# Mixer attention scores on 64 rows instead of 32, and three shifts in the traced order of a four-layer image kernel

## The chip, the cores and the metric

The kernel runs on one core of one Trainium2 chip. The metric is the device time of one execution in microseconds. TensorE is called PE here, VectorE DVE, ScalarE ACT, GpSimd POOL, and SyncE, which issues the DMAs, SP.

## The reference

Eight images of 256 channels by 32x32 (1024 tokens) go through four layers, each `x = x + layer(group_norm(x))` with 32 groups. Cut to what matters:

```python
# layer 0: attention, 8 heads of 64; q and k have unit length over the tokens
attn = softmax(einsum('bhdi,bhdj->bhij', q, k) * 10.0)
out = einsum('oc,bcxy->boxy', w_out, attn @ v) + b_out
# layers 1 and 2: 3x3 convolutions, 256 -> 256 channels
# layer 3
xn = layernorm(tokens of x)
xm = four branches of 64 channels: mamba(xn) + skip * xn   # a selective scan over the tokens
g  = sigmoid(conv1d(conv1d(xm)));  xg = g * xm
R  = pointwise(depthwise3(xg)) + xg
xm2 = pointwise(depthwise3(concat(x, R))) + x
x_local  = depthwise3(xm2)
x_global = mha(xm2)                                        # 8 heads of 32
t = gelu(layernorm(concat(x_local, x_global) @ fc.T + fc_b))
out = layernorm(depthwise 3x3 of ln_hw(t)) @ proj.T + proj_b
```

## The kernel before, in words

All data are float32, and channels lie on partitions: an image is two tiles of 128 x 1024. A Python program traces all instructions, and a scheduler with priorities then lays them out; each engine runs its own list strictly in that order. An instruction that waits therefore holds everything behind it on its engine.

There are two streams. `scan_layers` is the layer norm and the four scans of image b (64 units; a unit is a `drive` product on POOL, two `decays` on ACT, two `scan` steps on DVE, a `weigh` product on POOL and matmuls `y<-hs,sel` on PE). The other stream, `dense`, does for its neighbours what needs PE: `back_layers` of image b-1 (gate, projections, mixer attention), `front_attention` of image b+1 (layer 0), `back_out` of b-1, then `front_convs` of b+1 (the output projection of layer 0, in `project_both`, and both convolutions) with `back_end` of b-1 among them. `interleave` runs `dense` and sums the costs that it yields; each time the sum passes a multiple of `PACE[b]` (2.95 for most images) it traces one more step of the scans. `held` ties what is traced for the scans to the last dense instruction of the same engine ahead of it. `amid` gives the steps of `back_end` to places in the list of `front_convs`' yields. Those yields are numbered from 0: 0 to 3 are the output projection, 4 the group norm of convolution 1, 5 to 16 its twelve weight loads, 17 the group norm of convolution 2, 18 to 29 its loads.

Image 0's first layers come before the first scan, and the last image's mixer and end come after the last scan. Six stages between have all of the above; the one after them has the scans of the last image and only the mixer and the end of the image before.

An attention is cut in units: `scores` is a pair of heads' matmuls into one PSUM tile `big`, ACT takes `exp` of it into `p`, and two units later `values` multiplies `p` with v into `acc`. There are two `big` tiles and twelve work tiles (pool `tp`) for everything of size 128 x 1026. In layer 0 (`front_attention`) a pair is two heads of 64 rows, so the scores' operands lie on rows 0 to 63 and 64 to 127. In the mixer (`mixer_attention`) a pair is heads i and i+1, with operands of 32 rows:

```python
rows = [slice((j % 4) * 32, (j % 4) * 32 + 32) for j in (i, i + 1)]
...
"q": [qk[t][r, 0:N] for r in rows],
"k": [qk[2 + t][r, 0:N] for r in rows],
```

All four projections q0, k0, q1, k1 (`qk`, four work tiles) are made ahead of the first unit, and the local depthwise convolution (`local`, two work tiles) ahead of the attention. A head's sums and outputs come out of `acc` through `both` and DMAs; the division by the sums is in `invert`.

A group norm takes `channel_stats` on DVE (`st`, `mv`), two small matmuls with `gmat`, a chain of thirteen small DVE operations (`inverse_root`), and two ACT operations that write the padded images `im`. A layer norm over channels takes matmuls with `mean_w`, squares on ACT, the matmuls `acc<-mean_w,ln_sq`, a chain on DVE (`ln_r`) and matmuls with `ident`. In `back_end` the 3x3 depthwise convolution is 16 DVE steps ("taps", `dw<-xo,vec,dw`), followed by a layer norm whose mean is the matmul `big<-dw,mean_w`.

Of the kernel before, what the change touches and what calls it, by code (L numbers as in the profile page):

```python
# [19 lines left out]
P = 128  # L20
# [13 lines left out]
def preact_stack(ctx: ExitStack, tc: tile.TileContext, I, out, cols):  # L34
# [185 lines left out]
    fc_w = wdp.tile([2, P, 4, P], F32, tag="fc_w", name="fc_w")  # L220
    half_d = wp.tile([P, NB], F32, name="half_d")
    vector.tensor_scalar_mul(half_d, vec[:, cols["mD"] : cols["mD"] + NB], 0.5)
    half_qb = wp.tile([P, 2], F32, name="half_qb")
    vector.tensor_scalar_mul(
        half_qb, vec[:, cols["qpwb"] : cols["qpwb"] + 2], 0.5
# [144 lines left out]
    def inner(t):  # L370
        return t[:, 1 : N + 1]
# [683 lines left out]
    def mixer_attention(x2, img, exact=False):  # L1055


        v = vp.tile([P, NKT, 8, 64], F32, tag="v", name="v3")
        vector.memset(v[:, :, :, 32:64], 1.0)
        wv = chunk("ainv", 0)  # L1060
        for kt in range(0, NKT, 4):
            ps = big_tile()
            for i in range(4):
                for c in range(2):
                    tensor.matmul(
                        ps[:, i * C : (i + 1) * C],
                        inner(x2[c])[:, (kt + i) * P : (kt + i + 1) * P],
                        wv[:, c],
                        start=c == 0,
                        stop=c == 1,  # L1070
                    )
            vector.tensor_copy(
                v[:, kt : kt + 4, :, 0:32],
                ps.rearrange("p (k a b) -> p k a b", k=4, b=32),
            )
            yield 3.8

        qk = {}
        for t in (0, 2, 1, 3):
            qk[t] = work("qk3")  # L1080
            w = chunk("ainqk", t)
            ps = big_tile()
            for h in range(2):
                for c in range(2):
                    tensor.matmul(
                        ps[:, HALVES[h]],
                        w[:, c],
                        inner(x2[c])[:, HALVES[h]],
                        start=c == 0,
                        stop=c == 1,  # L1090
                    )
            scale = 32.0**-0.5 if t < 2 else 1.0
            vector.tensor_scalar(
                qk[t][:, 0:N], ps, col("ain_b", t), scale, ALU.add, ALU.mult
            )
            yield 3.4

        o = img["o3"] = [work("o3_0"), work("o3_1")]

        def head(i):  # L1100
            t, rows = i // 4, slice((i % 4) * 32, (i % 4) * 32 + 32)

            def take(half, acc):

                vector.tensor_copy(o[t][rows, half], acc)

            return {
                "q": qk[t][rows, 0:N],
                "k": qk[2 + t][rows, 0:N],
                "v": lambda kt: v[:, kt, i, 0:32],  # L1110
                "rows": rows,
                "take": take,
            }

        if exact:
            attention_exact(head(i) for i in range(8))
            return

        sums = {}

        def pair(i):
            t = i // 4
            rows = [slice((j % 4) * 32, (j % 4) * 32 + 32) for j in (i, i + 1)]

            def v_of(j):
                return lambda kt: v[:, kt, j]

            def take(h, acc, _):
                if t not in sums:
                    sums[t] = dp.tile([4, N], F32, tag="sums4", name="sums")  # L1130
                both = half_work("both")
                scalar.copy(both, acc)
                for e in range(2):
                    j, at = (i + e) % 4, e * 64
                    nc.sync.dma_start(
                        out=o[t][rows[e], HALVES[h]], in_=both[at : at + 32]
                    )
# [4 lines left out]
                if i % 4 == 2 and h == 1:  # L1142
                    ot = o[t][:, 0:N]

                    return invert(
                        sums[t], 4, 32, lambda r: vector.tensor_mul(ot, ot, r)
                    )

            return {
                "q": [qk[t][r, 0:N] for r in rows],  # L1150
                "k": [qk[2 + t][r, 0:N] for r in rows],
                "v": [v_of(i), v_of(i + 1)],
                "take": take,
            }

        yield from attention([lambda i=i: pair(i) for i in range(0, 8, 2)], False)

    def back_layers(img, exact=False, begin=None):

        xm = img.pop("xm")  # L1160

        q4 = work("q4")
        ps = big_tile()
        for h in range(2):
            for j in range(2):
                tensor.matmul(
                    ps[0:96, HALVES[h]],
                    qdw[:, j].rearrange("p k n -> p (k n)"),
                    inner(xm[j])[:, HALVES[h]],
                    start=j == 0,  # L1170
                    stop=j == 1,
                )
# [12 lines left out]
        yield 4  # L1185
        for j in range(2):
            ps = big_tile()
            for h in range(2):
                tensor.matmul(
                    ps[:, HALVES[h]],  # L1190
                    qpr[:, 2 * j : 2 * j + 2].rearrange("q b m -> q (b m)"),
                    q4[0:96, HALVES[h]],
                    start=True,
                    stop=True,
                )

            gate = work("gate")[:, 0:N]
            scalar.activation(
                gate, ps, AF.Tanh, bias=half_qb[:, j : j + 1], scale=0.5
            )  # L1200
            part = inner(xm[j])
            vector.scalar_tensor_tensor(part, gate, 1.0, part, ALU.add, ALU.mult)
        yield 3.4
        xt = load_x(img["xd"])


        rd = [work("rd0"), work("rd1")]
        for t in range(2):
# [12 lines left out]


        xs = [work("xs0"), work("xs1")]
        for t in xs:
            zero_ends(t)
        group_norm(xt, img["stats"], [inner(t) for t in xs])
        fd = []
        for t, src in enumerate(xs + r):
            fd.append(work("fd"))
            depthwise3(fd[t][:, 0:N], src, "fdw_w", "fdw_b", t)  # L1230
        x2 = [work("x20"), work("x21")]
        for t in x2:
            zero_ends(t)

        def evac_x2(m, ps):
            vector.scalar_tensor_tensor(
                inner(x2[m]), ps, col("fpw_b", m), inner(xs[m]), ALU.add, ALU.add
            )

        yield from project("fpw", fd, evac_x2)  # L1240


        local = [work("local0"), work("local1")]
        for t in range(2):
            depthwise3(local[t][:, 0:N], x2[t], "lc_w", "lc_b", t)
        for n, cost in enumerate(mixer_attention(x2, img, exact)):
            yield cost
            if n == 58 and begin is not None:
                next(begin)
        img["mix"] = xt, local  # L1250

    def merge_weights():
# [164 lines left out]
    def amid(stream, other, places):  # L1417
# [6 lines left out]
            yield cost  # L1424
        yield from other

    def slow(stream):

        for cost in stream:
            yield SLOW * cost  # L1430

    SLOW = 0.35
    PACE = [1.8] + [2.95] * (batch - 2) + [1.6]
    imgs = [{} for _ in range(batch)]
    drain(
# [3 lines left out]
    for b in range(batch):  # L1439

        def dense():
# [12 lines left out]
            if front is None:  # L1454
# [147 lines left out]
```

## Time and profile before

| What | Value |
|---|---|
| Time, three runs | 6783.45, 6793.21, 6796.24 us; median 6793.21 |
| Run of the profile | 6773.59 us, span 6771.8 us |
| Granted PE clock over the span | 0.859 |
| POOL products, `drive` and `weigh` | 512 each, 2568 and 2509 ns |
| DVE scan step | 1024, 1207 to 1265 ns |
| ACT `exp` of a unit | 1024, 1020 ns |
| Convolution matmuls | 2304, 1072.6 us busy |

The profile is one execution. Busy times are of an engine; idle time ahead of an instruction is put down to what released it last. The granted clock says what share of the full TensorE clock the chip's throttle let through. One float32 matmul of the source is two instructions in the profile. All instructions on PE, ACT and DVE that go through the kernel's wrapper `Paced` bear its line, L102; they are told apart by the tiles that they write and read.

### The profile page before, as it was taken

Reading aid. Unit: us, or ns where it says so; the run is one execution under the profiler, and the core shown is the slowest. Engines: PE = TensorE matmul, PEld = TensorE weight load, DVE = VectorE, ACT = ScalarE, POOL = GpSimd, SP = SyncE. Lnnn points to the kernel's source line nnn. Section 1 sums busy time; section 2 is a strip of 40 time slices with the busy share of each in tenths; the row PEclk is TensorE's granted clock in tenths of the full one; section 3 lists DMA queues with packets and bytes.
Section 4 is the critical chain, followed back from the end, with each engine's and each line's share of the span. In section 5 each row is a group of like instructions: output and inputs, shape, how many; then the busy total and the mean of one; then the engine's idle time right before and its main releaser. Section 6 shows DMA issues by size and latency. Waiting matters only on the chain.

```text
span 6771.8 us, 52155 instructions
## 1 busy us (share of the span) xinstructions
PE 5753.1 (85%) x17310; PEld 1933.1 (29%) x17310; DVE 3974.1 (59%) x4610; ACT 2690.7 (40%) x3225; POOL 2685.5 (40%) x1297
## 2 busy tenths in 40 slices
PE   8887688987998979998889888898799987978586
PEld 2331133222422234222332223322242223411132
DVE  4257745578545775467744775557854577545532
ACT  3234324543354433544235442454324452334232
POOL 0026652534344352633515334253434534265500
PEclk9987897998988979799888988789888998966697
DMA  1013232322233122221223222232222312223200
GB/s 49 27 59 84 77 83 67 90 57 75 72 89 86 47 76 78 73 80 48 84 66 91 64 62 79 69 87 57 70 77 70 104 39 82 77 69 89 80 19 30
DMA packets 216688, 470.81 MB, mean 70 GB/s; under 512 B 60116, under 2 KB 101716, under 8 KB 214360
## 3 DMA queue, kind: packets, MB, share of 16 engines
q1 hardware_dynamic: 216408, 467.38, 24.4%
q8 instruction: 139, 2.28, 0.1%
q14 instruction: 141, 1.16, 0.1%
HBM read 394.31 MB, written 64.49 MB: 68 GB/s over the span
## 4 chain that ended last, share of the span: by engine, by line
PE 59%; DVE 23%; issue 5%; ACT 5%; DMA 4%; POOL 2%; SPq 1%; DVEq 0%; POOLq 0%; ACTq 0%
PE big L102 37%; PE acc L102 14%; PE da L102 6%; DVE p L102 6%; DVE hs L102 5%; PE y L102 3%; DVE dw L102 2%; DVE t L102 2%; POOL hs L942 1%; DVE u L102 1%; DVE dt L102 1%; POOL hs L974 1%; DMA dt<-dt_m 1%; DVE st L102 1%; ACT p L102 1%
## 5 line engine op out<-in xcount | busy, mean ns | idle before, releaser
L942 POOL TENSOR_TENSOR hs<-du,bc 128x1024 f32<-128x1024 f32 x512 | 1307.7, 2568 | 1632.6 <-DMA dt<-dt_m 1296.5
L974 POOL TENSOR_TENSOR hs<-hs,bc 128x1024 f32<-128x1024 f32 x512 | 1284.3, 2509 | 835.2 <-DVE hs L102 762.5
L102 ACT ACTIVATE p<-big 128x1024 f32<-128x1024 f32 x1024 | 1038.6, 1020 | 1000.8 <-PE big L102 977.4
L102 PE MATMUL acc<-p,v 128*64 128x512 f32 x4096 | 1261.0, 688 | 29.5 <-ACT o L102 27.0
L102 PE MATMUL big<-im,w 128*128 128x512 f32 x2304 | 1072.6, 622 | 54.2 <-ACT im L102 36.7
L102 ACT ACTIVATE da<-dt,a_neg 128x512 f32<-128x512 f32 x1024 | 689.8, 687 | 888.9 <-DVE hs L102 673.0
L102 DVE TENSOR_TENSOR p<-p 128x1024 f32<-128x1024 f32 x448 | 793.0, 1770 | 296.9 <-ACT p L102 169.7
L102 DVE TENSOR_TENSOR_SCAN hs<-da,carry,hs 128x512 f32<-128x512 f32 x512 | 625.4, 1265 | 332.2 <-POOL hs L942 216.7
L102 DVE TENSOR_TENSOR_SCAN hs<-da,hs 128x512 f32<-128x512 f32 x512 | 598.9, 1207 | 375.9 <-POOL hs L942 221.5
L102 PE MATMUL big<-qk,qk 32*128 32x512 f32 x2048 | 734.6, 769 | 31.5 <-ACT p L102 29.2
L102 PE MATMUL big<-q,k 64*128 64x512 f32 x2048 | 604.6, 661 | 68.5 <-ACT p L102 40.9
L102 PEld LDWEIGHTS big<-im,w 128*128 128x128 f32 x2304 | 448.5, 199 | 696.1 <-issue 615.6
L973 POOL COPY carry<-hs 128x2 f32<-128x2 f32 x256 | 104.7, 409 | 1294.8 <-DVE hs L102 1279.4
L102 PE MATMUL y<-hs,sel 128*32 128x512 f32 x2048 | 409.3, 700 | 204.4 <-POOL hs L974 204.3
L102 PEld LDWEIGHTS acc<-p,v 128*64 128x64 f32 x4096 | 226.6, 146 | 930.0 <-issue 810.1
L102 PEld LDWEIGHTS big<-qk,qk 32*128 32x128 f32 x2048 | 191.2, 216 | 566.6 <-issue 260.6
L102 PE MATMUL big<-xn,w 128*128 128x512 f32 x512 | 255.7, 657 | 60.0 <-DMA w<-in_wqk 29.0
L102 PEld LDWEIGHTS big<-q,k 64*128 64x128 f32 x2048 | 163.1, 191 | 496.2 <-issue 260.2
L102 DVE SCALAR_TENSOR_TENSOR dw<-xo,vec,dw 128x961 f32<-128x961 f32 (+1 forms) x128 | 227.4, 1806 | 29.8 <-ACT dw L102 29.1
L102 PE MATMUL da<-xn,w_minw 64*128 64x512 f32 x256 | 150.7, 705 | 81.5 <-DVE hs L102 80.9
L102 PE MATMUL big<-o,w 128*128 128x512 f32 x384 | 189.6, 646 | 11.4 <-DVE o L102 11.4
L102 DVE SCALAR_TENSOR_TENSOR u<-raw,vec,u 128x1024 f32<-128x1024 f32 x96 | 136.5, 1422 | 106.4 <-ACT u L102 105.2
(205 smaller groups left out, 4975.3 us busy)
## 6 DMA issues: line engine op xcount, KB each, us to landing
bc<-bc SPq DMA_DIRECT2D x1024, 128.0 KB
dt<-dt_m SPq DMA_DIRECT2D x512, 128.0 KB
du<-du_m SPq DMA_DIRECT2D x512, 128.0 KB
w<-in_wc SPq DMA_DIRECT2D x192, 192.0 KB
rs<-inv SPq DMA_DIRECT2D x64, 256.0 KB
dt_m<-dt SPq DMA_DIRECT2D x64, 256.0 KB
du_m<-a SPq DMA_DIRECT2D x64, 256.0 KB
xt<-in_x SPq DMA_DIRECT2D x8, 1024.0 KB
```

The source lines that it names most:

```text
L102: made = issue(*args, **kwargs)
L942: nc.gpsimd.tensor_mul(u["hs"], u["du"], both_groups(u["bc"][:, 0]))
L973: nc.gpsimd.tensor_copy(carry[:, u["q"], g : g + 2], hs[:, :, HALF - 1])
L974: nc.gpsimd.tensor_mul(hs, hs, both_groups(u["bc"][:, 1]))
```

## The change

There are four edits.

- **Masked q, 64 rows.** The mixer makes two copies of q instead of one: `q[0]` holds the even groups of 32 rows and zeros in the odd ones, `q[1]` the reverse (a per-row factor `alt` of the usual scale or zero; DVE writes one copy and ACT the other). A pair is now heads i and i+2, and a score multiplies 64 rows of k, those of two heads, with 64 rows of masked q, of which 32 are zero. The sum is that of one head. The pairs are 0, 1, 4, 5 instead of 0, 2, 4, 6.
- **q and k of the second half later.** `q_and_k(1)` is traced when the attention first asks for pair 4, eight units before it is due, instead of ahead of the attention. The places of `begin` in the list of yields move by the two yields that so go.
- **Local convolution later.** Its two halves are traced at yields 34 and 40 of the mixer.
- **Lull, and a later image end.** `lull` holds back the cost of yields 0 to 3 and 15 to 16 of `front_convs` and passes it on with the next yield, so no scan step is traced there. The steps of `back_end` have new places in the same list.

```diff
-        for t in (0, 2, 1, 3):
-            qk[t] = work("qk3")
...
+        def q_and_k(t):
+            for at in (t, 2 + t):
...
+                if at == t:
+                    q = [work("qk3")[:, 0:N] for _ in range(2)]
+                    vector.tensor_scalar(
+                        q[0], ps, col("ain_b", t), alt[:, 0:1], ALU.add, ALU.mult
+                    )
+                    scalar.activation(
+                        q[1], ps, AF.Identity, bias=alt_b[:, t, 1:2], scale=alt[:, 1:2]
+                    )
+                else:
+                    k = work("qk3")[:, 0:N]
+                    vector.tensor_scalar_add(k, ps, col("ain_b", at))
+                yield 3.4
+            qk[t] = q, k
+        yield from q_and_k(0)
...
+            if t not in qk:
+                drain(q_and_k(t))
+            q, k = qk[t][0][i % 2], qk[t][1]
...
-                "q": [qk[t][r, 0:N] for r in rows],
-                "k": [qk[2 + t][r, 0:N] for r in rows],
-                "v": [v_of(i), v_of(i + 1)],
+                "q": [q[e * 64 : e * 64 + 64] for e in range(2)],
+                "k": [k[e * 64 : e * 64 + 64] for e in range(2)],
+                "v": [v_of(i), v_of(i + 2)],
...
-        yield from attention([lambda i=i: pair(i) for i in range(0, 8, 2)], False)
+        yield from attention([lambda i=i: pair(i) for i in (0, 1, 4, 5)], False)
...
-        local = [work("local0"), work("local1")]
-        for t in range(2):
+        local = []
+        def add_local():
+            t = len(local)
+            local.append(work("local"))
             depthwise3(local[t][:, 0:N], x2[t], "lc_w", "lc_b", t)
         for n, cost in enumerate(mixer_attention(x2, img, exact)):
             yield cost
-            if n == 58 and begin is not None:
+            if n in (34, 40):
+                add_local()
+            if n == 56 and begin is not None:
                 next(begin)
...
+    def lull(stream, spans):
+        owed = 0.0
+        for n, cost in enumerate(stream):
+            if any(a <= n < b for a, b in spans):
+                owed += cost
+                yield 0.0
+            else:
+                yield cost + owed
+                owed = 0.0
...
+    LULLS = (0, 4), (15, 17)
...
             yield from amid(
-                front_convs(imgs[b + 1]),
+                lull(front_convs(imgs[b + 1]), LULLS),
                 back_end(last, out[b - 1]),
-                (0, 4, 6, 7, 8, 9, 10, 11, 12, 13, 14, 16, 17, 20, 22, 25),
+                (5, 6, 8, 9, 10, 11, 12, 13, 14, 15, 16, 18, 20, 22, 24, 26),
             )
```

More of the change, by code (lines that the diff above doesn't have):

```diff
@@ L222, in preact_stack @@
     vector.tensor_scalar_mul(half_d, vec[:, cols["mD"] : cols["mD"] + NB], 0.5)
+    alt = wp.tile([P, 2], F32, name="alt")
+    nc.gpsimd.memset(alt, 0.0)
+    for g in range(4):
+        nc.gpsimd.memset(alt[g * 32 : g * 32 + 32, g % 2 : g % 2 + 1], 32.0**-0.5)
+    alt_b = wp.tile([P, 2, 2], F32, name="alt_b")
+    for t in range(2):
+        vector.tensor_scalar_mul(alt_b[:, t], alt, col("ain_b", t))
     half_qb = wp.tile([P, 2], F32, name="half_qb")
@@ L1078, in mixer_attention @@
         qk = {}
-        for t in (0, 2, 1, 3):
-            qk[t] = work("qk3")
[L1081 to L1090, printed above, removed]
-                    )
[L1092 to L1096, printed above, removed]
+        def q_and_k(t):
+            for at in (t, 2 + t):
+                w = chunk("ainqk", at)
+                ps = big_tile()
+                for h in range(2):
+                    for c in range(2):
+                        tensor.matmul(
+                            ps[:, HALVES[h]],
+                            w[:, c],
+                            inner(x2[c])[:, HALVES[h]],
+                            start=c == 0,
+                            stop=c == 1,
+                        )
[3 more added lines that the diff above has]
+                        q[0], ps, col("ain_b", t), alt[:, 0:1], ALU.add, ALU.mult
+                    )
+                    scalar.activation(
[7 more added lines that the diff above has]
+        yield from q_and_k(0)
         o = img["o3"] = [work("o3_0"), work("o3_1")]
@@ L1105, in take @@
                 vector.tensor_copy(o[t][rows, half], acc)
+            if t not in qk:
+                drain(q_and_k(t))
             return {
-                "q": qk[t][rows, 0:N],
-                "k": qk[2 + t][rows, 0:N],
+                "q": qk[t][0][i % 2][rows],
+                "k": qk[t][1][rows],
                 "v": lambda kt: v[:, kt, i, 0:32],
@@ L1122, in pair @@
             t = i // 4
-            rows = [slice((j % 4) * 32, (j % 4) * 32 + 32) for j in (i, i + 1)]
+            if t not in qk:
+                drain(q_and_k(t))
+            q, k = qk[t][0][i % 2], qk[t][1]
             def v_of(j):
@@ L1133, in take @@
                 for e in range(2):
-                    j, at = (i + e) % 4, e * 64
+                    j, at = i % 4 + 2 * e, e * 64
                     nc.sync.dma_start(
-                        out=o[t][rows[e], HALVES[h]], in_=both[at : at + 32]
+                        out=o[t][j * 32 : j * 32 + 32, HALVES[h]],
+                        in_=both[at : at + 32],
                     )
@@ L1141, in take @@
                     )
-                if i % 4 == 2 and h == 1:
+                if i % 4 == 1 and h == 1:
                     ot = o[t][:, 0:N]
@@ L1247, in back_layers @@
             yield cost
-            if n == 58 and begin is not None:
+            if n in (34, 40):
+                add_local()
+            if n == 56 and begin is not None:
                 next(begin)
+        while len(local) < 2:
+            add_local()
         img["mix"] = xt, local
```

## The prediction

> **What bounds the kernel now.** I read the page first: engines, granted clock, chain.
>
> ```profile
> span 6771.8 us, 52155 instructions
> PE 5753.1 (85%) x17310; PEld 1933.1 (29%) x17310; DVE 3974.1 (59%) x4610; ACT 2690.7 (40%) x3225; POOL 2685.5 (40%) x1297
> PEclk9987897998988979799888988789888998966697
> PE 59%; DVE 23%; issue 5%; ACT 5%; DMA 4%; POOL 2%; SPq 1%; DVEq 0%; POOLq 0%; ACTq 0%
> ```
>
> TensorE (PE) carries the end: 85% busy, 59% of the chain, and not always at full clock (0.859 over the span). DVE is the other 23%. The groups show the two kinds of scores:
>
> ```profile
> L102 PE MATMUL big<-qk,qk 32*128 32x512 f32 x2048 | 734.6, 769 | 31.5 <-ACT p L102 29.2
> L102 PE MATMUL big<-q,k 64*128 64x512 f32 x2048 | 604.6, 661 | 68.5 <-ACT p L102 40.9
> ```
>
> As many matmuls, with as much streamed, cost 130 us more in the mixer (32 rows) than in the image attention (64 rows). By stretch, in this order: a mixer with scans, an image attention, the last mixer with scans, the mixer after the scans, the convolutions. Columns: length, busy time and count of PE, PEld, DVE, ACT, POOL, granted clock, DMA share, GB/s.
>
> ```profile
> 1896.00:2106.00 210.00, 196.22 (x623) 44.23 (x624) 94.04 (x93) 115.19 (x140) 120.78 (x65) 0.80 0.32 88
> 2157.00:2347.00 190.00, 171.41 (x620) 45.38 (x618) 139.54 (x137) 94.71 (x114) 57.48 (x23) 0.97 0.19 53
> 5924.00:6294.00 370.00, 299.68 (x732) 61.03 (x728) 174.33 (x142) 155.10 (x195) 231.11 (x118) 0.66 0.28 76
> 6531.00:6661.00 130.00, 129.68 (x503) 31.42 (x504) 3.00 (x5) 68.04 (x71) 0.00 (x0) 1.00 0.05 12
> 1560.00:1814.00 254.00, 212.52 (x583) 92.97 (x582) 162.37 (x204) 67.52 (x82) 121.30 (x59) 0.86 0.26 79
> ```
>
> The mixer has LESS idle than the attention (13.8 against 18.6 us) and yet a clock of 0.80 against 0.97. With no scans and no idle, 32-row scores keep clock 1.00. So 32 rows are not slow in themselves; they fail to get the clock back once it is lost. One stretch inside the first mixer, then the timeline of each kind at work:
>
> ```profile
> 1906.40:1947.30 40.90, 39.89 (x82) 7.40 (x80) 15.89 (x12) 15.03 (x19) 19.28 (x12) 0.51 0.15 40
> ```
>
> ```profile
> 1909.40 1.98 PE L102 MATMUL acc<-p,v 128*64 128x512 f32 x4
> 1911.30 2.08 PE L102 MATMUL big<-qk,qk 32*128 32x512 f32 x4
> 1913.31 1.98 PE L102 MATMUL acc<-p,v 128*64 128x512 f32 x4
> ```
>
> PE is busy 39.89 of 40.90 us at half clock, a unit (scores and values) taking 3.9 us. The attention at full clock takes 2.07 us a unit (scores 1.06, values 1.01), and mixer units at full clock take the same. The last view is PE in a convolution stage:
>
> ```profile
> 1587.46 0.59 PE L102 MATMUL acc<-mv,gmat 128*128 128x4 f32 x2 [7.92 <-DVE mv L102]
> 1669.77 1.02 PE L102 MATMUL big<-dw,mean_w 128*128 128x512 f32 x2
> 1678.63 3.78 PE L102 MATMUL da<-xn,w_minw 64*128 64x512 f32 x4 [7.84 <-DVE hs L102]
> 1687.69 4.21 PE L102 MATMUL big<-dw,mean_w 128*128 128x512 f32 x6 [5.28 <-DVE dw L102]
> ```
>
> PE waits 7.92 us for the statistics before the first group norm, and 13.1 us in the middle of convolution 1, because the image end's mean matmul stands there before its DVE taps are done.
>
> [...]half-clock spells here last multiples of 3.41 us[...] the spell above lasted 40.96 us, busy throughout.[...] a pair of scores still runs side by side; the trace agrees (four instructions in 1.06 us either way).[...] taps here take 1187 ns at the least and up to 3339.
>
> **The change part by part.** The sum is against the profiled span, 6771.8 us; its run took 6773.6, the three others 6783 to 6796.
>
> 1. *64-row scores.* Removed: nothing on PE, the matmul count stays. Six mixers run beside scans, lasting 210.9, 209.5, 219.5, 219.1, 219.5, 212.8 us between first and last score (mean 215.2). Their full-clock work is (210.0-13.8) x 0.80 = 157 us each. At the attention's clock, a little lower for the scans' waits (0.95), 157/0.95 = 165; plus idle of 22 (now 14 to 17, the attention 18; it grows because POOL, 120 us in 210, has less time): 187. Gain 28 x 6 = 168; bounds 10 and 35 each. The seventh (370.5 us, clock 0.66, 70 idle) is paced by scans: 46 units of scan in it; a stretch of the second mixer did 8 units in 53 us, 6.6 each, so 305 at best, and 325 taken: gain 45, bounds 15 and 65. The last, already at 1.00: nothing.
>    Added: a second masked q copy, on ACT, 2 per image x 8; the nearest PSUM row on ACT (`xo<-big`) is 1.11 us, so 18 us of ACT, which is 40% busy; its reader comes a pair (16 units) later. It holds its PSUM buffer no longer than DVE's 1.28 us copy beside it. Bounds 0 to 1 us each. The setup's five memsets and two small DVE operations lie under the first loads.
> 2. *Second q and k inside the attention.* PE's 7 us are moved, not added; a bubble of about 1 us at the PSUM buffers, as the attention's own waits (16.4 us in 24 on `ACT big`), against 7 us earlier start of exp. The four weight loads stand where they stood on SP. Zero; bounds -1 and +3 per image.
> 3. *Local convolution later.* Four DVE steps of 1.28 and two of 1.24 on ACT leave the start of the mixer, where PE waits 2.76 us for `x`, and go where DVE is under half busy. 2 us x 7 = 14; bounds 0 and 3.
> 4. *Image end later.* The build order shows the mean matmul after convolution 2 has begun, its taps before convolution 1's last statistics. The 13.1 us go. But all 16 taps now lie before those statistics: from the tap start to there DVE has about 29 us of taps (16 x 1.8), 14 of scans, 5 of others, 48, against about 50 of PE work: some of the wait returns at the second group norm, 4 taken. Both `ln_sq` sums leave the group norms' wait, where DVE's chain sat 6.5 us behind them; PE loses that filling (7 us cold), and does it warm elsewhere (32 matmuls took 4.1 us at full clock): +3. On SP the image's load goes five yields later, the stores one; the x buffer they free is wanted one step later than before: bounds 0 to 3.
> 5. *Lull.* Statistics without scans between: the three scan steps (1.2 each) and `dt` ahead of `mv` go: from 8 to about 5 us. Filling for PE is gone, so the two group norms idle 8.5 us each against 16.6 together before: zero. What is held (13.8 and 10.4 of cost, at 2.95 a step 4.7 and 3.5 steps, each with its SP loads, ACT decays, DVE scans, POOL products, PE sums) arrives in a burst: PE sums may wait for POOL: 2 taken, 0 to 20. Parts 4 and 5: 13.1-4+3-2 = 10 us x 6 images = 60; bounds -5 and 20 each.
>
> Sum: 168+45+14+60 = 287, so 6485 by the span; from the median, 6793-287 = 6506. I say 6510.
>
> **Rivals.** *Zeros don't count* (half the masked q is zero[...]): the mixers stay at 0.80, parts 3 to 5 remain: 6793-74 = 6719. For it: the trace has no 64-row scores with zeros. Against: [...] all that the trace shows goes with shapes. *Scans become the bound*: the clock rises but PE idles on POOL: mixers gain 10 each, 60+15+14+60 = 149: 6644. For: POOL ran no better than 62% in the two stages that scans pace. Against: 6.6 us a unit was reached. *Bursts after the lulls, slower*: the owed 8.2 steps are 4.1 units, 21 us of POOL at 5.1, right after both group norms; PE stands behind a sum,[...] and the convolutions, whose DVE is full of taps, wait again. It decides from 287-60 = 227/6 = 38 us an image; at 45, 6793-227+270 = 6836. Against: only 21 us are owed, and taps were seen to fit. *The change doesn't do what it says*: the order shows 64-row instructions and the new places; only the time is open.
>
> **How the numbers follow.** As forecast 0.71 (its own range 6420 to 6600), scans the bound 0.13, zeros 0.12, bursts 0.04. A measurement of this kernel can tell some 0.2% (14 us) from no change. Faster 0.94, same 0.02, slower 0.04. The range, 6410 to 6660, takes in the scan case and leaves out the zeros, the bursts and the ends of the first.
>
> **What would show it.** Mixers beside scans of 180 to 195 us at clock 0.92 or more, half-clock spells of one or two windows; fewer than 75 us saved in all with mixers at 0.80 would mean zeros. In the convolutions no `dw,mean_w` wait; if `y` waits on POOL pass 30 us an image (now 12), the bursts are real. A mixer at clock 0.95 but idle over 35 us makes the scans the bound. A span over 6660 proves me wrong.

## The result, and the profile after

The changed kernel takes 6684.76 us (median of four runs, 6672.71 to 6691.39) against 6788.33 us before (four runs, 6768.15 to 6796.24): a ratio of 0.985, 95% interval 0.9823 to 0.9877. It is faster, as forecast, but by about 103 us where 283 were forecast, and 25 us above the top of the range. Medians of the kernel before, taken anew beside each group of experiments, range from 6781 to 6800 us, so kernels are compared below by their ratio to it, and 0.001 of ratio is 6.8 us. Where a text says "by the spans", it compares single profiled executions; such a difference is up to some 20 us off that of the ratios.

The page of the changed kernel, the same lines as before:

```profile
span 6680.2 us, 52240 instructions
PE 5489.3 (82%) x17310; PEld 1854.4 (28%) x17310; DVE 4001.5 (60%) x4612; ACT 2721.9 (41%) x3253; POOL 2723.7 (41%) x1302
PEclk9988798998989989999899998999889897988697
PE 55%; DVE 25%; issue 6%; DMA 5%; ACT 5%; POOL 3%; SPq 1%; DVEq 0%; POOLq 0%; ACTq 0%
```

PE is busy for 264 us less and the clock over the span rose from 0.859 to 0.891, but the span fell by only 92: PE idles more. The stretches in the same order as before (a mixer with scans, an image attention, the last mixer with scans, the mixer after the scans), and last a convolution stage, here cut from its first to its last matmul:

```profile
1890.00:2097.00 207.00, 179.02 (x624) 43.57 (x624) 100.85 (x94) 114.86 (x138) 120.50 (x61) 0.90 0.31 86
2155.00:2333.00 178.00, 168.22 (x621) 44.91 (x622) 136.92 (x136) 95.01 (x114) 53.92 (x21) 0.98 0.17 50
5886.00:6201.00 315.00, 240.65 (x732) 53.18 (x732) 160.60 (x141) 155.02 (x193) 216.48 (x111) 0.84 0.35 92
6429.00:6566.00 137.00, 136.52 (x518) 34.63 (x520) 9.40 (x11) 71.52 (x74) 0.00 (x0) 1.00 0.05 12
2374.00:2617.00 243.00, 190.54 (x542) 79.90 (x543) 159.00 (x176) 67.14 (x83) 127.99 (x61) 0.85 0.27 79
```

The mixer's clock went from 0.80 to 0.90, the last scan stage's from 0.66 to 0.84: the 64 rows did what they were to do. But the mixer's idle doubled (13.8 to 28.0 us), and in the convolution stage PE is idle for 52 us (30 before, from first to last matmul). What PE waits for there is in the waits of PE, by cause; first before, then after (total us, times, longest):

```profile
PE y L102 <- POOL hs L974: 204.3, 59, 9.8
...
PE big L102 <- DVE dw L102: 88.5, 9, 29.0
PE big L102 <- ACT p L102: 76.9, 39, 13.5
PE acc L102 <- DVE mv L102: 73.9, 15, 7.9
...
PE big L102 <- ACT im L102: 36.7, 16, 6.9
```

```profile
PE big L102 <- DMA w<-in_wc: 253.1, 8, 40.3
PE y L102 <- POOL hs L982: 153.5, 52, 21.8
PE big L102 <- ACT p L102: 128.1, 54, 12.3
PE big L102 <- ACT im L102: 85.4, 16, 6.9
...
PE big L102 <- DMA w<-fc_w: 65.1, 7, 10.1
PE acc L102 <- DVE mv L102: 48.7, 15, 3.7
...
PE big L102 <- DVE dw L102: 31.1, 2, 29.0
```

The wait for the mean matmul (`dw`) is gone from the six stages, and a wait for a convolution weight (`w<-in_wc`) has come: some 39 us once in each. A second new one is for the weights `fc_w` behind the mixer, 10 us each. The wait for the padded images `im`, ahead of the convolutions, has grown by 49 us in all.

Both spans cut into stretches at the first matmul of each kind, and summed over the images, in us, with experiment e3 (the mixer's edits alone) between them:

| Stretch | before | e3 | after |
|---|---|---|---|
| six mixers beside scans, to the next image's v | 1307 | 1261 | 1272 |
| ahead of all eight mixers (projection `fpw`, v, first q and k) | 344 | 292 | 292 |
| last mixer beside scans | 404 | 351 | 351 |
| mixer after the scans | 132 | 139 | 139 |
| layer 0's v, eight images | 159 | 134 | 133 |
| layer 0's first q and k with `back_out`, six images | 177 | 221 | 222 |
| six image attentions and output projections | 1440 | 1379 | 1314 |
| six convolution stages | 1290 | 1299 | 1456 |
| gate | 301 | 304 | 288 |
| all else | 1201 | 1202 | 1196 |
| sum (without some 18 us ahead of the first) | 6754 | 6581 | 6662 |

So by these spans the mixer's edits gave 173 us. The other edits, lull and later image end, took 81 of them back (191 and 89 by the ratios): the convolution stages grew by 157, the stretch ahead of them shrank by 65.

### The profile page after: what moved, and what is told of

Its sections match the earlier page's. It is cut to its first block, busy times and chain, and to the rows that moved or that the text cites. A ratio compares the mean times of both kernels' runs of the same rounds, so it can differ in the third digit from the quotient of the medians.

```text
span 6680.2 us, 52240 instructions
## 1 busy us (share of the span) xinstructions
PE 5489.3 (82%) x17310; PEld 1854.4 (28%) x17310; DVE 4001.5 (60%) x4612; ACT 2721.9 (41%) x3253; POOL 2723.7 (41%) x1302
## 4 chain that ended last, share of the span: by engine, by line
PE 55%; DVE 25%; issue 6%; DMA 5%; ACT 5%; POOL 3%; SPq 1%; DVEq 0%; POOLq 0%; ACTq 0%
PE big L102 36%; PE acc L102 11%; DVE p L102 6%; DVE hs L102 6%; PE da L102 5%; PE y L102 3%; DVE u L102 2%; POOL hs L982 2%; DVE t L102 2%; POOL hs L950 2%; DVE dw L102 1%; DVE dt L102 1%; DMA dt<-dt_m 1%; DVE y L102 1%; DVE st L102 1%
## 5 line engine op out<-in xcount | busy, mean ns | idle before, releaser
L982 POOL TENSOR_TENSOR hs<-hs,bc 128x1024 f32<-128x1024 f32 x512 | 1327.0, 2592 | 1013.3 <-DVE hs L102 951.0
L102 PE MATMUL big<-im,w 128*128 128x512 f32 x2304 | 1096.9, 630 | 338.5 <-DMA w<-in_wc 253.1
L102 PE MATMUL acc<-p,v 128*64 128x512 f32 x4096 | 1167.4, 640 | 0.7 <-ACT o L102 0.7
L102 DVE TENSOR_TENSOR p<-p 128x1024 f32<-128x1024 f32 x448 | 777.0, 1734 | 271.4 <-ACT p L102 183.3
L102 PE MATMUL big<-qk,qk 64*128 64x512 f32 x2048 | 655.0, 674 | 105.9 <-ACT p L102 94.1
L102 PE MATMUL y<-hs,sel 128*32 128x512 f32 x2048 | 408.8, 723 | 153.7 <-POOL hs L982 153.5
L102 PEld LDWEIGHTS big<-qk,qk 64*128 64x128 f32 x2048 | 178.0, 195 | 570.9 <-issue 298.3
L102 DVE SCALAR_TENSOR_TENSOR dw<-xo,vec,dw 128x992 f32<-128x992 f32 (+1 forms) x128 | 227.4, 1824 | 27.3 <-ACT dw L102 26.7
L102 PE MATMUL big<-xn,w 128*128 128x512 f32 x512 | 232.6, 608 | 6.7 <-ACT p L102 6.7
L102 DVE SCALAR_TENSOR_TENSOR xt<-big,vec,xt 128x1024 f32<-128x1024 f32 x48 | 61.4, 1280 | 226.9 <-PE big L102 226.9
L102 DVE SCALAR_TENSOR_TENSOR u<-raw,vec,u 128x1024 f32<-128x1024 f32 x96 | 150.1, 1564 | 64.4 <-ACT u L102 63.9
```

Of the source, the lines that this page charges most:

```text
L102: made = issue(*args, **kwargs)
L982: nc.gpsimd.tensor_mul(hs, hs, both_groups(u["bc"][:, 1]))
```

## The experiments

**Edits apart: lulls and places.** Five kernels take the changed kernel and undo one lull or both, the image end's new places, or lulls and places.

e3, the mixer's edits alone:

```diff
-    LULLS = (0, 4), (15, 17)
+    LULLS = ()
...
-                (5, 6, 8, 9, 10, 11, 12, 13, 14, 15, 16, 18, 20, 22, 24, 26),
+                (0, 4, 6, 7, 8, 9, 10, 11, 12, 13, 14, 16, 17, 20, 22, 25),
```

> The changed kernel without lulls and with the image end's old places: the mixer's edits alone. All theories: no wait for weights; mixers and stages ahead of them as in the changed kernel (17 us an image less than before, 55 in the stage of the last scans), convolution stages as before, with 13 us for dw,mean_w and statistics at 8 us. Theory A: 6772 - 6 x (17 + 10) - 55 - 10, about 6540 by the span. If the shorter stage of layer 0 came from the lull, the 10 goes and it is 6600.

Measured: 6597.23 us, ratio 0.9719 (0.9687 to 0.9752). Without lulls and new places it is 1.3% faster than the changed kernel. The time is the expectation's 6600: the shorter stage of layer 0 did come from the lull.

e5, new places without lull:

```diff
-    LULLS = (0, 4), (15, 17)
+    LULLS = ()
```

> The changed kernel without any lull; the image end's later places are kept. Beside the mixer's edits alone (6599 by the span) this adds the places alone. If the first lull alone makes the wait for weights, there is none and it is 6590 to 6610. If the later places make it by themselves (taps ahead of the scans on DVE, the scans' loads ahead of the weights on SP), some 20 us an image of it stay: 6640 or more.

Measured: 6625.96 us, 0.9746 (0.9716 to 0.9776). The new places alone cost some 18 us by the ratio, with intervals that overlap, and 31 by the spans; a convolution stage takes 222.4 us (216.4 in e3). The time lies between the two numbers expected. The weights' wait is there without any lull:

```profile
PE big L102 <- DMA w<-in_wc: 172.4, 14, 21.3
PE y L102 <- POOL hs L982: 135.6, 34, 21.8
```

In e3 these two are 18.5 and 235.2 us. So the new places bring 26 us of wait for a weight to each of the six stages, two thirds of the changed kernel's, mostly in place of the waits for the scans' sums `y` and for `dw,mean_w`.

e6, both lulls with the old places:

```diff
-                (5, 6, 8, 9, 10, 11, 12, 13, 14, 15, 16, 18, 20, 22, 24, 26),
+                (0, 4, 6, 7, 8, 9, 10, 11, 12, 13, 14, 16, 17, 20, 22, 25),
```

> The changed kernel with both lulls and the image end's old places. In the order on SP the seventh weight of convolution 1 now stands ahead of the second round of scan loads. If the wait needs both edits: no wait for weights, 6590 to 6620. If the lull costs by itself, through its burst on POOL and DVE: 6650 or more.

Measured: 6714.08 us, 0.9882 (0.9854 to 0.991). Here the lulls cost 0.0163, some 111 us: they cost by themselves.

e1 and e2, one lull each with the new places:

```diff
-    LULLS = (0, 4), (15, 17)
+    LULLS = ((15, 17),)
```

> The changed kernel with the lull at yields 15 and 16 alone; yields 0 to 3 (the output projection) give scan steps again. Theory A (the burst that the first lull owes puts dt, du and bc loads of the scans ahead of the seventh weight of convolution 1 on SP, and these wait for the scans): no wait for in_wc of over 5 us in the six full stages, so some 6 x 40 = 240 us less than the changed kernel, about 6450. Theory B (the image end's later places fill DVE with taps, the scans wait for DVE, and so do the loads): the wait stays, about 6680. Theory C (the weights are slow to land, since the burst's transfers fill the DMA engines): the burst at convolution 2 is left, half of the wait stays, about 6560.

```diff
-    LULLS = (0, 4), (15, 17)
+    LULLS = ((0, 4),)
```

> The changed kernel with the lull at yields 0 to 3 alone. Theory A: the order on SP ahead of the seventh weight is that of the changed kernel, so the wait of 39 us an image stays: 6680 within 25. Theory B: the same. Theory C: less than half of the wait is left only if the second burst had a part in it; else 6680.

Measured: the second lull alone 6619.77 us, 0.9762 (0.9728 to 0.9796), not to be told from no lull; the first alone 6691.34 us, 0.9863 (0.983 to 0.9895), not to be told from both. In e1 none of the three theories' numbers held (the wait for `in_wc` is 149.5 us, near that of e5). The first lull, which holds back four yields and gives 13.8 of cost back at the group norm of convolution 1, is the one that costs.

**Rows alone.** e7 is e3 with 32-row operands cut out of the same tiles; the order of instructions is that of e3, but for some swapped neighbours (19 pairs of 17310 on PE, two on DVE).

```diff
+            rows = [slice(j * 32, j * 32 + 32) for j in (i % 4, i % 4 + 2)]
...
-                "q": [q[e * 64 : e * 64 + 64] for e in range(2)],
-                "k": [k[e * 64 : e * 64 + 64] for e in range(2)],
+                "q": [q[r] for r in rows],
+                "k": [k[r] for r in rows],
```

> The mixer's edits alone, but each score takes only the 32 rows of its own head, from the same tiles; every engine's order is the same as with 64 rows. Theory clock (rows bring back the clock): mixers beside scans at a clock of 0.78 to 0.82, 20 to 30 us longer each, the stage of the last scans 40 us longer: 6599 + 6 x 25 + 40, about 6790. Rival (the gain came from moving q, k and the local convolution): 6600 within 25, clocks as with 64 rows.

Measured: 6748.68 us, 0.9939 (0.9915 to 0.9963): in e3's order the rows alone are worth 151 us. The clocks are those of the clock theory, its time was 40 us too long; the rival is refuted. A mixer beside scans and the mixer after them, in e7 and then in e3:

```profile
1881.00:2096.00 215.00, 199.00 (x625) 46.50 (x626) 100.69 (x95) 115.13 (x138) 120.66 (x61) 0.81 0.30 84
6455.00:6634.00 179.00, 178.56 (x518) 41.66 (x520) 9.39 (x10) 71.54 (x73) 0.00 (x0) 0.75 0.04 9
```

```profile
1883.00:2087.00 204.00, 175.81 (x626) 43.41 (x628) 101.20 (x95) 114.81 (x139) 121.08 (x62) 0.92 0.31 88
6348.00:6485.00 137.00, 136.27 (x516) 34.44 (x516) 9.65 (x11) 71.46 (x73) 0.00 (x0) 1.00 0.05 12
```

The last mixer has no idle in either. With 32 rows it fell to half clock just after its start, and stayed there for 26 windows of 3.41 us (89 us) at 99.8% busy; with 64 rows it never left full clock. So being busy did not by itself bring the clock back in these 26 windows. In the mixer beside scans the clock was 0.81 with 32 rows and 0.92 with 64; columns were not varied.

By stretch, e7 is longer than e3 by 73 us in the six mixers beside scans, 43 in the last scan stage and 42 in this last mixer. The kernel before, with 32 rows too, lost nothing in its last mixer (clock 1.00), so these 42 us don't come from the rows alone: e7 has other pairs of heads, and PE idles 1.8 us at that mixer's start, where it idled 0.3 before. Which of the two it is was not tried.

**Zeros.** e9 is e3 with the scale in all rows of `alt`. It leaves the masking out, so each score sums two heads.

```diff
-    nc.gpsimd.memset(alt, 0.0)
-    for g in range(4):
-        nc.gpsimd.memset(alt[g * 32 : g * 32 + 32, g % 2 : g % 2 + 1], 32.0**-0.5)
+    nc.gpsimd.memset(alt, 32.0**-0.5)
```

> The changed kernel without lull and with the old places (its median was 6597 us), but the factor alt holds the scale in all rows, so that both copies of q are whole and no zero enters the scores: each score sums two heads, which leaves the masking out and changes the output; every instruction keeps its shape and its place. Theory A (the clock follows shapes and busy time, what the data are does not matter): 6590 to 6610 us, mixer clock 0.90 to 0.92. Theory B (rows that multiply zeros count less): the mixers reach a higher clock with whole data, 0.95 or more, and the time falls by over 30 us, to under 6565.

Measured: 6603.24 us, 0.9717 (0.9692 to 0.9742), mixer clock 0.90 to 0.93 (0.92 in e3). Zeros cost no clock here: theory A.

**Second q and k, local convolution.** e8 is e3 with `q_and_k(1)` ahead of the attention again (the places of `begin` and of the local convolution move with it by two yields), e10 is e3 with the local convolution there again.

```diff
-        yield from q_and_k(0)
+        for t in range(2):
+            yield from q_and_k(t)
```

> The mixer's edits alone, but with all of q and k made ahead of the attention as in the kernel before; the fc weights stand on SP where they stood before. If late q and k caused the new wait of 9.9 us an image for the fc weights: that wait goes, no bubble of big tiles in the mixer, and the mixer's start is 7 us later for the same work: 6599 - 7 x 8, about 6540. If the wait only moves to the next weights (in_wqk, 5 us before): 6570 to 6600.

```diff
+        add_local()
+        add_local()
         for n, cost in enumerate(mixer_attention(x2, img, exact)):
             yield cost
-            if n in (34, 40):
-                add_local()
```

> The changed kernel without lull and with the old places (6597 us), the local convolution's two halves back ahead of the mixer attention, where the kernel before has them. Theory A (the forecast's part 3: 2 us an image and up to 14 in all): 6605 to 6615 us, with a longer wait of PE for x or k at the start of the mixer. Theory B (its six steps are hidden in either place, or stand in the way of the attention's own DVE steps where they are now): within 7 us of 6597, or under it.

Measured: e8 6627.03 us, 0.9761 (0.973 to 0.979), e10 6596.82 us, 0.9703 (0.968 to 0.9727). Neither of e8's two numbers held. The late q and k gain about 29 us by the ratio (the intervals overlap) and 21 by the spans, though not in the mixer: there they add 59 us over six and take 43 away ahead of all eight. But the six image attentions with their output projections are 61 us shorter (PE idles 24 us in each and not 34), layer 0's v is 26 shorter, and 37 us come on around `back_out`, where the wait for `fc_w` comes up. The late local convolution gains nothing: theory B.

**What makes the convolution stage longer.** First the timeline of PE in the changed kernel, then that of the SP queue, at the same place:

```profile
2426.37 2.84 PE L102 MATMUL big<-im,w 128*128 128x512 f32 x6
2468.29 2.05 PE L102 MATMUL big<-im,w 128*128 128x512 f32 x2 [39.08 <-DMA w<-in_wc]
```

```profile
2439.09 0.88 SPq L937 DMA_DIRECT2D bc<-bc  x2
2450.88 11.66 SPq L927 DMA_DIRECT2D dt<-dt_m  x8
2462.64 1.76 SPq L927 DMA_DIRECT2D du<-du_m  x4
2464.49 0.37 SPq L156 DMA_DIRECT2D w<-in_wc  x1
```

The weight's load is issued at 2464.49 and takes 3.67 us. It stands on SP behind eight `dt` loads and four `du` loads of scan steps. That alone is not the lull's doing: in e5, without a lull, eight `dt` loads (issued from 2431.95 to 2441.53 us) stand ahead of a weight as well, and PE waits 20.5 us there. Each group waits for ACT to finish with the `dt` tile before, ACT (`da`) for a DVE scan, and the scan stands in DVE's list between taps of the image end. From the chain of waits there (start, us, what):

```profile
2440.70 2.37 ACT xo L102 x2
2443.08 1.14 ACT dw L102
2444.24 3.51 DVE dw L102 x3
2447.75 2.37 DVE hs L102 x2
...
2454.40 3.32 DVE dw L102
2457.73 2.38 DVE hs L102 x2
2460.13 0.70 ACT da L102
...
2464.49 3.67 DMA w<-in_wc
```

e4 takes the queue out of this chain: the weights of the convolutions are loaded from ACT's queue.

```diff
-        nc.sync.dma_start(out=t, in_=src[i])
+        queue = nc.scalar if name in ("wc1", "wc2") else nc.sync
+        queue.dma_start(out=t, in_=src[i])
```

> The changed kernel with the convolutions' weight loads issued from ACT's queue instead of SP's; all else in the same trace order. Theory A: the weights no longer stand behind scan loads, the 39 us an image go, though ACT now waits for weight buffers at places of its own: 6450 to 6550. Theory B: PE gets its weights but waits for the scans' sums and the taps instead: over 6620. Theory C: the weights land as late as now: 6680.

Measured: 6662.55 us, 0.9816 (0.9784 to 0.9849), against theory A. Its waits of PE:

```profile
PE y L102 <- POOL hs L983: 260.3, 102, 21.8
PE big L102 <- DMA w<-in_wc: 36.8, 6, 6.2
```

The wait for weights falls from 253.1 to 36.8 us, the wait of the scans' sums `y` rises from 153.5 to 260.3, and the stage gets 5 us shorter (237.7), which is theory B, but for the taps, for which PE doesn't wait there. The queue is where the delay shows; without that wait PE reaches the scans' sums before these are done, and stands there.

e13 gives the held cost back in parts instead of at once; e14 leaves every second tap of the image end out.

```diff
             else:
-                yield cost + owed
-                owed = 0.0
+                part = min(owed, 1.5)
+                yield cost + part
+                owed -= part
```

> The changed kernel (6685 us) with both lulls and the new places, but what a lull has held back is given back in parts of 1.5 with each of the following yields (nine of them after the first lull, seven after the second) and not in one sum. Theory A (the burst is the cause: four or five scan steps at once, with their SP loads and DVE steps, fall between the group norm and the convolution's last weight): the wait for in_wc falls under 20 us an image and the time to 6600 to 6635, where the kernel without lulls is (6626). Theory B (it is enough that these steps come in the convolutions instead of the stretch ahead of them, in whatever dose): within 20 us of 6685. Theory C (it is the SP queue alone, where a weight stands behind any load that waits): the wait stays over 30 us an image.

```diff
             for n, k in enumerate((0, 1, 2, 3, 5, 6, 7, 8)):
+                if n % 2:
+                    yield 1
+                    continue
...
-                if n % 2:
-                    yield 1
```

> The changed kernel (6685 us) with every second one of the 16 taps of the image end's convolution left out, which changes the output; the order of traced steps stays as it is. It takes 8 DVE instructions of about 1.8 us, 14 us of DVE, out of the convolution stage. Theory A (DVE's list, where taps and scan steps stand between one another, is what the dt loads and so the weights wait for in the end): the stage from the first convolution matmul to the last falls from 242 us to 222 to 230, the wait for in_wc from 39 to under 30 us an image, the time by 75 to 120 us, to 6565 to 6610. Theory B (the queue or POOL's products set it): the stage over 236, the time over 6650; what else is saved is the end of the last image, 14 us or so.

Measured: e13 6605.86 us, 0.9727 (0.9711 to 0.9744), as theory A said for the time; e14 6634.05 us, 0.9765 (0.9748 to 0.9781), between its two theories. The convolution stage of e13, from first to last matmul, and its SP queue ahead of the weight:

```profile
2363.00:2588.00 225.00, 181.81 (x511) 75.20 (x512) 144.79 (x173) 62.36 (x78) 132.87 (x61) 0.88 0.30 85
```

```profile
2431.29 1.70 SPq L927 DMA_DIRECT2D dt<-dt_m  x4
2433.03 0.42 SPq L937 DMA_DIRECT2D bc<-bc  x1
2433.55 0.37 SPq L156 DMA_DIRECT2D w<-in_wc  x1
2434.80 1.70 SPq L927 DMA_DIRECT2D dt<-dt_m  x4
```

As many POOL instructions (61) as in the changed kernel's stage, and 18 us less, of which 3 come back in the stretch ahead: what costs is not that the scan steps come there but that they come together. Now one group of `dt` stands ahead of the weight, not two. The wait for it is still 30.81 us here, so theory A's figure for the wait failed, and C's held, while C's cause (the queue alone) is against e4. What went with the burst is 8.0 us an image at `in_wc`, 7.0 at `im` and 2.4 at `y`. In e14 the taps take 13.8 us of DVE in a stage and not 31.9; the stage gets 9 us shorter (233.2) and the wait falls to 30.6 on average, just over the 30 expected: DVE's list is part of the chain, with half a microsecond for each that it is relieved of.

e16 puts the spread lulls on the old places (the `places` edit of e6 on e13):

```diff
-                (5, 6, 8, 9, 10, 11, 12, 13, 14, 15, 16, 18, 20, 22, 24, 26),
+                (0, 4, 6, 7, 8, 9, 10, 11, 12, 13, 14, 16, 17, 20, 22, 25),
```

> The old places of the image end with both lulls, which cost 117 us there when given back in one sum (6714 against 6597), now given back in parts of 1.5 a yield. Theory A (the burst is what costs, wherever the image end stands): 6575 to 6615 us, no wait for in_wc or y over 12 us an image more than without lulls. Theory B (the new places are what made the spread lull harmless, since taps and image-end matmuls come later there): over 6650.

Measured: 6649.6 us, 0.9796 (0.978 to 0.9813). Spreading takes 0.0086, 58 us, off e6; some 52 us over e3 stay. So with the old places the burst is half of what the lulls cost. Theory A's time failed, while its bound on the waits held; the median is, within the noise, at theory B's 6650. What the other half is was not tried; beside e3, PE waits some 60 us more for the scans' sums `y` and 28 more for `in_wc`.

**Weights behind the mixer, and the fastest version.** e11 is e3 with `fc_w` loaded from ACT's queue; e12 is e3 with the second lull.

```diff
-        nc.sync.dma_start(out=t, in_=src[i])
+        queue = nc.scalar if name == "fcw" else nc.sync
+        queue.dma_start(out=t, in_=src[i])
```

> The changed kernel without lull and with the old places (6597 us), the weights fc_w loaded from ACT's DMA queue, so that their loads no longer stand behind the scans' loads on SP. Theory A (the wait of 9.2 us an image for fc_w is on the path): it goes, and the time falls by 30 to 60 us, to 6540 to 6565. Theory B (the wait only shows where PE stands; the scans behind it set the end, as the conv weights did): under 15 us of gain, over 6582, and PE waits for something else in the same stretch.

```diff
-    LULLS = ()
+    LULLS = ((15, 17),)
```

> The changed kernel with old places of the image end and only the second lull, cost of yields 15 to 16 held back. With the new places this lull took 6 us from the time (6626 to 6620). Theory A (the lulls cost by what they hold back, and the first, which holds back four yields ahead of a weight load, is the one that costs; the second frees the statistics): 6580 to 6605 us. Theory B (with old places either lull puts scans between the taps, as both together cost some 117 us there): over 6630.

Measured: 6597.29 us, 0.9706 (0.9683 to 0.9729), and 6595.18 us, 0.9705 (0.968 to 0.973): both at e3's level, so theory B for e11 and A for e12. In e11 the wait is gone (7.6 us an image less in its stretch), 4.3 of that come back in the image attention, and the last stages, which have no image attention, lose 23 us in all. So e15 uses the ACT queue in the six stages alone, with the second lull; e17 does the same for e13.

```diff
+            early[0] = True
             yield from back_out(last)
+            early[0] = False
...
+        queue = nc.scalar if name == "fcw" and early[0] else nc.sync
+        queue.dma_start(out=t, in_=src[i])
```

> The changed kernel without the first lull and with the old places of the image end, with the second lull, and with the weights fc_w loaded from ACT's queue in the six stages that have an image attention (not in the last two, where it cost 50 us at the end and won 27 before it). Theory A (the shares that the stages of the runs before showed add up: 4 us an image from fc_w, 2 from the second lull): 6555 to 6580 us. Theory B (what a stage gains by an earlier weight it gives back as a wait for the scans, so that all these variants stand at one level): 6588 to 6602.

> The changed kernel with both lulls given back in parts of 1.5 (6606 us with the fc_w loads on SP), the new places, and fc_w from ACT's queue in the six stages. Theory A (the fc_w gain adds up as it did beside the second lull, 34 us): 6565 to 6585 us, so not ahead of the version with old places and second lull alone (6561). Theory B (the conv stage, where PE still waits over 30 us an image for its last weight, takes it back): over 6595.

Measured: e15 6561.24 us, 0.966 (0.9644 to 0.9676), e17 6568.77 us, 0.9676 (0.966 to 0.9693): theory A in both. e15 has the lowest median, 3.4% under the kernel before and 1.9 points of ratio under the changed one; e17 is not to be told from it.

## Why the prediction failed, step by step

The forecast was 287 us off the span; 92 came. The difference has one failed step and three terms of wrong size.

- **Parts 4 and 5, the failed step.** Forecast: "10 us x 6 images = 60". Measured: e3 to the changed kernel, 81 us of loss by the spans, so 141 us of the error. e5 tells the two parts apart.
  - *Part 4, the later image end*, was to gain 13.1 - 4 + 3 us an image, 72 in all. It cost 31 by the spans (18 by the ratio). The wait for `dw,mean_w` went, as forecast, and the wait for `y` with it. What failed is the term for SP: "On SP the image's load goes five yields later", "bounds 0 to 3", looked at the image's own load and stores and put nothing for the convolutions' weights. The wait for these weights is 26 us in each stage of e5. That the order on SP makes it is read from e5's trace; no run moved the weights there.
  - *Part 5, the lull*, was to cost 2 us an image, 12 in all. It cost 50 more by the spans (71 by the ratio). "PE sums may wait for POOL: 2 taken" priced the burst as POOL time and looked for it at `y`. Against e5, an image has 3.4 us more at `y`, but 13.5 at `w<-in_wc` and 5.5 at `im`. Each returned scan step also puts its `dt` and `du` loads on SP, ahead of the weights, and these wait for DVE through ACT. The burst is 83 us of ratio (the changed kernel to e13); that DVE's list and not the queue alone is behind the wait, e14 and e4 show.
  - Without the burst, parts 4 and 5 still gain nothing (e13 against e3: 6 us longer by the spans, within the noise). Some of what they were to gain was gone already: with the late q and k the waits for statistics `mv` fell from 73.8 us (e8) to 29.9 (e3), and those for `dw` from 88.5 to 70.5. In the changed kernel `mv` is 48.7: the lull did not shorten that wait.
- **The rival "bursts after the lulls"** was right in kind, with a chance of 0.04. It named the wrong wait (`y`), and put its price at 45 us an image. The convolution stage grew by 26 us over e3's, places and lulls together, and the stretch ahead of it, rid of those steps, gave 11 back (1379 to 1314 over six): far from the 38 net that it would have taken to make the kernel slower.
- **Part 1, right in cause, too large by about 60 us.** With 64 rows instead of 32 a mixer beside scans has a clock of 0.92 and not 0.81 (e3, e7), and zeros cost none of it (0.90 to 0.93 without them, e9), so that rival is refuted. e8, which has the q and k where they were, is 152 us shorter than the kernel before by the spans, where part 1 has 168 + 45 (part 3, which is in e8 too, gave nothing). The last scan stage was forecast at 325 us and took 324 there. The six mixers were forecast to gain 28 us each and gave 17.6 (1307 to 1202 over six): their idle is the 22.7 us that the prediction took as 22, so the term of the wrong size is the clock, 0.91 and not the 0.95 assumed. Spells at half clock still come, in the changed kernel five or six to a mixer, of one to three windows each (3.41 to 10.24 us), where there were four or five of up to twelve (40.96 us); what starts those that are left was not tried.
- **Part 2, taken as zero, gained** about 29 us by the ratio, 21 by the spans (e8 against e3), in the image attention. Why that attention idles less when the second q and k come late is open: in the second of the six stages the wait for the statistics ahead of the first norm (`mv`) falls from 7.9 to 2.1 us and that for the weights `in_wqk` from 4.9 to nothing, but no run tells why.
- **Part 3, forecast 14 us, gave nothing** that can be told from zero (e10).
- **"Scans become the bound"** is not what is missing. A mixer idles for 28 us in the changed kernel, not over the 35 set as its mark, most of it behind `p` and `u` (14 and 12 us). In e8, with the same 64 rows, these are 5 us and nothing: the two waits come with the late q and k.

Together, by the spans: 141 us from parts 4 and 5, 61 from part 1, 14 from part 3, less 21 from part 2, is the 195 us between 287 and 92. The sum closes because e8 and e3 are steps on the way from the kernel before to the changed one; how a step's loss divides into its waits is read from one profile each.

## What to carry to other kernels

Price a step that is moved by everything it issues, and look at everything that then stands behind it. Here the returned scan steps were as many on POOL as in e13, but they held DVE, ACT and the DMA queue in one chain, and a weight load stood at its end. The engine named in the wait was only the last link: another queue for these loads took most of the wait away and gave 22 us. Nor is a wait of PE a loss of time by itself: e13 waits 31 us an image for the weight and is not to be told in time from e3, which waits for none in these stages. Work held back from a stage should come back in small parts: giving some five steps back at once cost 83 us here over giving them back in parts (58 with the other places of the image end). Operands of 32 rows instead of 64 cost clock here (0.81 against 0.92 in a mixer beside scans, e7 and e3) and not time at full clock (a unit took 2.07 us with either): compare the granted clock of stretches that have equally little idle time.

## What the runs showed that was not expected

Many small DVE operations ended together with a POOL product. In the changed kernel 744 float32 operations of 128 x 2 with no large POOL product beside them take 0.16 us in the median; 86 that met one take 1.18 us, and up to 2.29. Of these, 65 take over 0.4 us, and each of the 65 ends within 0.03 us of the end of a product. Two more, int32 operations of the chain ahead of the image end's taps, and the POOL products at the time:

```profile
2425.39 2.27 DVE L102 TENSOR_SCALAR bits<-rs_hw 128x2 int32<-128x2 int32 x1
2427.69 2.27 DVE L102 TENSOR_SCALAR y<-bits 128x2 int32<-128x2 int32 x1
```

```profile
2425.28 4.65 POOL L950 TENSOR_TENSOR hs<-du,bc 128x1024 f32<-128x1024 f32 x2
```

Each ends as one of the two products does, within 0.03 us. Why they end together the trace does not show. A chain of thirteen small operations, with three of 2.25 to 2.27 us in it here, thus sets when the image end's taps can begin (the chain runs from 2424.29 to 2440.61 us, the first tap starts at 2444.24), in the very stage that had become too long.
